# The second layer's gate product made behind the gate, into the head's weighted input

## The chip, the cores and the metric

The program runs on one core of a Trainium2 chip. The metric is the device time of one execution in microseconds (us), the median of several runs. A profile is one further execution, taken by the hardware profiler: its span runs from the first to the last instruction, and its own time includes what lies around the span.

## The reference, cut to what matters

The program is a network of four layers in float32. The change lies in the second, which takes an image of 56 x 56 points (3136 tokens), two images of a batch, 128 channels. The channels are cut into four heads of 32, which are computed one behind another, since each takes the result of the one before as part of its input:

```python
chunks = jnp.split(x, 4, axis=3)
prev = _vss_block(chunks[0], p) + vss_skip * chunks[0]
outs = [prev]
for i in range(1, 4):
    s = prev + chunks[i]
    prev = _vss_block(s, p) + vss_skip * s
    outs.append(prev)
x_res = cvm_skip * x_orig + jnp.concatenate(outs, axis=3)
return _layernorm(x_res, final_ln_w, final_ln_b)

def _vss_block(x, p):
    return x + _ss2d(_layernorm(x, p['ln1_w'], p['ln1_b']), p)

def _ss2d(x, p):
    xx, z = jnp.split(x @ in_proj_w.T, 2, axis=-1)
    xx = silu(depthwise_conv_3x3(xx) + conv_b)
    y = ...                                   # four scans over the image
    y = _layernorm(y, out_norm_w, out_norm_b) * silu(z)
    return y @ out_proj_w.T
```

So a head's result is (1 + vss_skip) * s + ((y - mean) / sd * w + b) * silu(z) @ out_proj. The last term falls into two: one with w that needs y, and one with the norm's bias b, which is (b * silu(z)) @ out_proj and needs only the gate silu(z). This second product is what the change moves. In the data given b is zero and w is one, but the kernel takes both as inputs and computes both products.

## The kernel before, in words

Engines: PE is TensorE, DVE VectorE, ACT ScalarE, POOL GpSimd; SP issues the transfers.

The second layer is the class `Layer1`. A head's scans take both images at once: 2 x 64 inner channels fill 128 partitions, and 3136 tokens lie along the free axis. Between the scans of one head and those of the next lies a stretch of work in chunks of 448 tokens (8 rows of the image, 4 tiles of 112 tokens), seven chunks in all. Only these stretches are touched. There are five: one before the first head's scans, three between heads, and one behind the last head, in which the third layer also begins.

`run` sets the order of emission: for each head it emits the scans, then for c from 0 to 7 first `after(head - 1, c)`, which ends the head before, and then `before(head, c)`, which prepares the next. For head 0, `before` alone is called (through `start`), and behind head 3 `after` with the last normalisation (`last`) and the work that follows. The inside of the scans is an order written out by hand; the stretches between are put into each engine's queue by the compiler's scheduler, whose result differs from the order of emission.

Buffers that matter: `self.prev` holds the head's running input (tokens in the partitions; the profile calls it pair), `self.z` the gate in channel layout (also in a buffer named pair), `self.row` and `self.col` the convolution's results in two orders, `self.y` the scans' sum, `k.X` the layer's input and result (X). `self.R["vss_skip"]` already holds 1 + vss_skip. `self.outs[0]` and `self.outs[1]` are the output matrix multiplied by w and by b (outonw and outonb).

`before(head, c)`, by lines:

- L842: prev += X (the next head's input); L78 to L86: its norm over 32 channels, with DVE, ACT and, at L86, POOL.
- L848, L849: POOL multiplies X by cvm_skip and prev by 1 + vss_skip. `after` later adds the head's product to it.
- L852: four transposes of nrm into a PSUM tile pt; L853: ACT copies it to hT; L855: in-projection of the convolution's half; L856: ACT writes it into the padded image pad.
- `conv_rows` for chunk c - 1 (it needs the row below): on DVE as one L464 and eight L466, or on PE as nine matmuls with diagonal weights (L460; 18 passes in the trace, an f32 matmul being two). Then L467 (silu, ACT) and L468 (POOL, a transposed copy). In heads 1 to 3 the calls c = 2, 4, 5, 6 are DVE's and 1, 3, 7 PE's; in head 0, 2 to 6 are DVE's.
- L867: in-projection of the gate's half; L868: silu into z.
- After c == 2 the first steps of the next scans are begun.

`after(head, c)`: L881 squares y (ACT), L883 multiplies y by the gate (POOL, yc), L888 makes the gate's product with outs[1], L890 the variance, L892 the product of yc with outs[0], L894 and L895 the reciprocal deviation; then on DVE L899 u = p2 + prev, L903 t = p1 * rs, L907 prev = t + u, and on POOL L908 X += prev. In head 3, POOL adds X to u (L901) and L905 writes t + u into X.

PSUM: [...] `pmid1` holds two of each of pt, p and pv (one for head 0, where only pt is used); `pcon1` has two pcv. In SBUF the pool mid1 has two of each of its tiles.

Behind a stretch, the next scans' first broadcast (L364, PE) and product (L417, DVE) start the scan (L358, DVE).

Of the kernel before, what the change touches and what calls it, by code (L numbers as in the profile page):

```python
# [14 lines left out]
F32 = mybir.dt.float32  # L15
BF16 = mybir.dt.bfloat16
AF = mybir.ActivationFunctionType
ALU = mybir.AluOpType
# [3 lines left out]
B = 2  # L22
# [3 lines left out]
TP = 112  # L26
NT = L // TP
CH = 448
# [42 lines left out]
def layernorm_tokens(k, out, x, sq, st, d, by=None, last="POOL"):  # L71

    nc = k.nc
    g = x.shape[1]
    mean, var = st[:, 0, :], st[:, 1, :] if by is None else by
    nc.vector.tensor_reduce(mean, x, AX.X, ALU.add)  # L78
    nc.vector.tensor_scalar_mul(mean, mean, 1.0 / d)
    nc.vector.tensor_tensor(out, x, mean.unsqueeze(2).to_broadcast([TP, g, d]), ALU.subtract)  # L80
    nc.scalar.activation(sq, out, AF.Square)
    nc.vector.tensor_reduce(var, sq, AX.X, ALU.add)
    nc.scalar.activation(var, var, AF.Sqrt, bias=k.eps[:TP], scale=1.0 / d)
    nc.vector.reciprocal(var, var)
    if last == "POOL":
        nc.gpsimd.tensor_tensor(out, out, var.unsqueeze(2).to_broadcast([TP, g, d]), ALU.mult)  # L86
    else:
        for i in range(g):
            nc.scalar.activation(out[:, i], out[:, i], AF.Copy, scale=var[:, i : i + 1])
# [21 lines left out]
class Scans:  # L111
# [290 lines left out]
    def emit(self, s):  # L402
        nc = self.k.nc
        now, one, two, three = (self.at(s + i) for i in range(4))
        before, done = self.at(s - 1), self.at(s - 2)
        if s == len(self.steps) + 2:
            self.take_out(self.steps[-1]["job"])
# [5 lines left out]
        if before:  # L413
            self.keep(before)
# [31 lines left out]
def conv_rows(k, pools, pad, diag, taps, bias, row, col, c, by):  # L446


    nc = k.nc
    sp, pp = pools  # L450
    cs = slice(CH * c, CH * (c + 1))

    def shifted(t):
        dy, dx = divmod(t, 3)
        return pad[:, 8 * c + dy : 8 * c + dy + 8, dx : dx + HW]

    if by == "PE":
        s = pp.tile([128, CH], F32, name="pcv")
        for t in range(9):
            nc.tensor.matmul(s, lhsT=diag[:, t, :], rhs=shifted(t), start=t == 0, stop=t == 8)  # L460
    else:
        s = sp.tile([128, CH], F32, name="cv")
        v = s.rearrange("p (r w) -> p r w", w=HW)
        nc.vector.tensor_scalar(v, shifted(0), taps[:, 0:1], None, ALU.mult)  # L464
        for t in range(1, 9):
            nc.vector.scalar_tensor_tensor(v, shifted(t), taps[:, t : t + 1], v, ALU.mult, ALU.add)  # L466
    nc.scalar.activation(row[:, cs], s, AF.Silu, bias=bias)  # L467
    nc.gpsimd.tensor_copy(  # L468
        col.rearrange("p (w h) -> p w h", h=HW)[:, :, 8 * c : 8 * c + 8],
        row[:, cs].rearrange("p (h w) -> p w h", w=HW),  # L470
    )
# [87 lines left out]
def layer0(k, d, big, follow):  # L559
# [3 lines left out]
    with ExitStack() as ctx:  # L563
# [46 lines left out]
        with ExitStack() as sctx:  # L610
# [87 lines left out]
            for b in range(B):  # L698
                with ExitStack() as bctx:
# [23 lines left out]
                    for c in range(NCH + 1):  # L723
                        if b == 0 and c == 2:
                            norm(1, (ap, tp), groups)
                        if b > 0 and c < NCH:
                            after(b - 1, (sp, pp, ip), c, *outs)
                        before(b, (sp, cp), c, pads, diag)
                        if c == 2:
                            scans.first(cp)  # L730
                scans.run()
        with ExitStack() as bctx:
            sp = bctx.enter_context(k.pool("midl", 2))
            pp = bctx.enter_context(k.pool("pmidl", psum=True))
            ip = bctx.enter_context(k.pool("onel"))
            outs = outputs(ip)
            chunk = follow(bctx)
            for c in range(NCH + 1):
                if c < NCH:
                    after(B - 1, (sp, pp, ip), c, *outs)  # L740
                chunk(c)


class Layer1:
# [4 lines left out]
    D = 32  # L749
# [80 lines left out]
    def before(self, head, pools, c, pad):  # L830


        k, nc, D, W = self.k, self.k.nc, self.D, self.W
        sp, pp, vp = pools
        cs = slice(CH * c, CH * (c + 1))
        if c < NCH:
            sv = self.chunk(self.prev, c)
            xs = self.chunk(self.channels(head), c)
            if head == 0:
                nc.vector.tensor_copy(sv, xs)  # L840
            else:
                nc.vector.tensor_tensor(sv, sv, xs, ALU.add)  # L842
            nrm = sp.tile([TP, 4, B * D], F32, name="nrm")
            nv = nrm.rearrange("p j (b c) -> p (j b) c", c=D)
            sq = sp.tile([TP, 4 * B, D], F32, name="sq")
            st = sp.tile([TP, 2, 4 * B], F32, name="st")
            layernorm_tokens(k, nv, sv, sq, st, D)
            nc.gpsimd.tensor_scalar(xs, xs, self.R["cvm_skip"], None, ALU.mult)  # L848
            nc.gpsimd.tensor_scalar(sv, sv, self.R["vss_skip"], None, ALU.mult)  # L849
            pt = pp.tile([2 * D, CH], F32, name="pt")  # L850
            for i in range(4):
                nc.tensor.transpose(pt[:, TP * i : TP * (i + 1)], nrm[:, i], k.ident[:TP, :TP])  # L852
            nc.scalar.copy(self.hT[:, cs], pt)  # L853
            ps = vp.tile([128, CH], F32, name="pcv")
            nc.tensor.matmul(ps, lhsT=W["in_w"][:, 0, :], rhs=self.hT[:, cs], start=True, stop=True)  # L855
            nc.scalar.activation(  # L856
                pad[:, 1 + 8 * c : 9 + 8 * c, 1 : 1 + HW], ps.rearrange("p (r w) -> p r w", w=HW),
                AF.Identity, bias=self.inb[:, 0:1],
            )
        if c > 0:  # L860
            conv_rows(
                k, (sp, vp), pad, self.diag, W["taps"], W["conv_b"], self.row, self.col, c - 1,
                "DVE" if c in ((2, 3, 4, 5, 6) if head == 0 else (2, 4, 5, 6)) else "PE",
            )
        if c < NCH:
            ps = vp.tile([128, CH], F32, name="pcv")
            nc.tensor.matmul(ps, lhsT=W["in_w"][:, 1, :], rhs=self.hT[:, cs], start=True, stop=True)  # L867
            nc.scalar.activation(self.z[:, cs], ps, AF.Silu, bias=self.inb[:, 1:2])  # L868
        if c == 2:
            self.scans.first(vp)  # L870

    def after(self, head, pools, c):

        k, nc, D = self.k, self.k.nc, self.D
        sp, pp = pools
        cs = slice(CH * c, CH * (c + 1))
        y, gate = self.y[:, cs], self.z[:, cs]
        sq = sp.tile([128, CH], F32, name="sq0")  # L880
        nc.scalar.activation(sq, y, AF.Square)  # L881
        yz = sp.tile([128, CH], F32, name="yc0")
        nc.gpsimd.tensor_tensor(yz, y, gate, ALU.mult)  # L883
        p = pp.tile([TP, 2, 4, B * D], F32, name="p")
        pv = pp.tile([TP, 4 * B], F32, name="pv")
        tiles = [slice(TP * i, TP * (i + 1)) for i in range(4)]
        for i, ts in enumerate(tiles):
            nc.tensor.matmul(p[:, 1, i], lhsT=gate[:, ts], rhs=self.outs[1], start=True, stop=True)  # L888
        for i, ts in enumerate(tiles):
            nc.tensor.matmul(pv[:, B * i : B * (i + 1)], lhsT=sq[:, ts], rhs=self.mean, start=True, stop=True)  # L890
        for i, ts in enumerate(tiles):
            nc.tensor.matmul(p[:, 0, i], lhsT=yz[:, ts], rhs=self.outs[0], start=True, stop=True)  # L892
        rs = sp.tile([TP, 4 * B], F32, name="rs")
        nc.scalar.activation(rs, pv, AF.Sqrt, bias=k.eps[:TP])  # L894
        nc.vector.reciprocal(rs, rs)  # L895
        p1, p2 = (p[:, i].rearrange("p j (b c) -> p (j b) c", c=D) for i in range(2))
        s, x = self.chunk(self.prev, c), self.chunk(self.channels(head), c)
        u = sp.tile([TP, 4 * B, D], F32, name="u")
        nc.vector.tensor_tensor(u, p2, s, ALU.add)  # L899
        if head == 3:  # L900
            nc.gpsimd.tensor_tensor(u, u, x, ALU.add)  # L901
        t = sp.tile([TP, 4 * B, D], F32, name="t")
        nc.vector.tensor_tensor(t, p1, rs.unsqueeze(2).to_broadcast([TP, 4 * B, D]), ALU.mult)  # L903
        if head == 3:
            nc.vector.tensor_tensor(x, t, u, ALU.add)  # L905
        else:
            nc.vector.tensor_tensor(s, t, u, ALU.add)  # L907
            nc.gpsimd.tensor_tensor(x, x, s, ALU.add)  # L908

    def last(self, sp, c):  # L910
# [548 lines left out]
class Mixer:  # L1459
# [104 lines left out]
    def into(self, by, place, onto=None):  # L1564
# [3 lines left out]
        for outs in sorted(by, key=len):  # L1568
            ps = self.product(by[outs])
            for o in outs:  # L1570
# [4 lines left out]
                else:  # L1575
                    nc.vector.tensor_tensor(place(o), onto(o), ps, ALU.add)

    def unit(self, f0, eo, after, later, project):


# [463 lines left out]
```

## Time and profile before

| what | value |
|---|---|
| median of 3 runs (lowest, highest) | 9105.64 us (9102.32, 9109.07) |
| the profiled execution's own time | 9098.37 us |
| its span | 9096.6 us |
| PE busy (share of the span) | 7993.2 us (88%) |
| PE weight loads | 4765.5 us (52%) |
| DVE busy | 7088.0 us (78%) |
| POOL busy | 6350.1 us (70%) |
| ACT busy | 3854.8 us (42%) |
| moved by DMA | 1362.92 MB |
| the stretch before head 0's scans | 2748.7 to 2883.7 us, 135.0 us |
| the stretch head 0 to 1 | 3519.5 to 3615.9 us, 96.4 us |
| the stretch head 1 to 2 | 4248.9 to 4345.6 us, 96.7 us |
| the stretch head 2 to 3 | 4983.4 to 5079.7 us, 96.3 us |
| the end of head 3's last scan | 5719.0 us |

The busy shares are averages over four layers with different limits. The stretches that the change touches are some 6% of the span, so these shares say little on it; the windows cut at the scans do. The ends of a stretch are taken as the end of a head's last scan instruction (L358) and the start of the next head's first.

### The profile page before, as it was taken

The page shows a single profiled execution, that of the slowest core. Times are in us where ns is not written, and L with a number is a line of the kernel's source. Part 1 is how long each engine was busy: PE and PEld are TensorE (multiplying, and loading weights), DVE is VectorE, ACT ScalarE, POOL GpSimd, SP SyncE. Part 2 cuts the span into 40 slices and gives each one's busy share as a digit, 9 for nine tenths or more (in the row PEclk, how much of TensorE's full clock was granted, in tenths as well). Part 3 has the DMA queues.
Part 4 walks back from the last instruction along what each step waited for, and adds up shares of the span by engine and source line. Part 5 has one row for each costly group of instructions (what it writes and reads, how often), then busy time and mean ns, then how long its engine had stood idle before and what let it go on. Part 6 is the DMA issues. An engine that isn't in the chain of part 4 may idle for free. (4 is left out here: it accounts for less than half of the span.)

```text
span 9096.6 us, 93496 instructions
## 1 busy us (share of the span) xinstructions
PE 7993.2 (88%) x28687; PEld 4765.5 (52%) x28687; DVE 7088.0 (78%) x7568; ACT 3854.8 (42%) x6644; POOL 6350.1 (70%) x4066
## 2 busy tenths in 40 slices
PE   8888888888887888888888888699999999999998
PEld 4444445444444444444444444355688888874555
DVE  8999998999997997998999899511467667665442
ACT  4555545555555555554554555433211111114331
POOL 6999996999996997998899799566311111115551
PEclk9999999999999998998999899799999999999999
DMA  5666664666664995996898699100233333320004
GB/s 159 221 221 220 222 212 127 221 221 220 222 220 110 230 226 134 227 228 157 203 227 204 157 227 224 39 3 3 85 96 105 104 94 110 93 63 8 14 1 135
DMA packets 780368, 1362.92 MB, mean 150 GB/s; under 512 B 133101, under 2 KB 405486, under 8 KB 779834
## 3 DMA queue, kind: packets, MB, share of 16 engines
q1 hardware_dynamic: 779866, 1356.95, 53.1%
q8 instruction: 227, 3.72, 0.2%
q14 instruction: 275, 2.25, 0.1%
HBM read 1317.03 MB, written 39.60 MB: 149 GB/s over the span
## 5 line engine op out<-in xcount | busy, mean ns | idle before, releaser
L430 POOL TENSOR_TENSOR p<-h,c 128x784 f32<-128x784 f32 x2048 | 3761.2, 1864 | 115.0 <-DVE h L358 33.1
L358 DVE TENSOR_TENSOR_SCAN h<-a,state,h 128x784 f32<-128x784 f32 x1536 | 2791.8, 1840 | 51.6 <-ACT a L339 28.7
L378 PE MATMUL acc<-p,center 128*128 128x392 f32 x4096 | 1499.0, 499 | 22.7 <-POOL p L430 20.8
L378 PE MATMUL acc<-p,ident 128*128 128x392 f32 x4096 | 1491.9, 498 | 6.7 <-POOL p L430 6.7
L417 DVE TENSOR_TENSOR h<-du,b 128x784 f32<-128x784 f32 x1408 | 1336.7, 949 | 75.6 <-PE b L364 70.4
L339 ACT ACTIVATE a<-delta,L0A 128x784 f32<-128x784 f32 x1024 | 939.3, 918 | 973.4 <-DVE h L358 971.5
L339 ACT ACTIVATE a<-delta,L1A 128x784 f32<-128x784 f32 x1024 | 939.2, 917 | 908.3 <-DVE h L358 905.3
L364 PE MATMUL b<-three,sel 96*128 96x512 bf16 (+1 forms) x2816 | 728.6, 341 | 563.9 <-DVE h L417 460.1
L433 POOL TENSOR_TENSOR h<-du,b 128x784 f32<-128x784 f32 x640 | 1190.3, 1860 | 4.1 <-PE pcv L460 4.1
L378 PEld LDWEIGHTS acc<-p,center 128*128 128x128 f32 x4096 | 740.9, 192 | 536.8 <-POOL p L430 60.2
L378 PEld LDWEIGHTS acc<-p,ident 128*128 128x128 f32 x4096 | 743.9, 192 | 512.8 <-POOL p L430 26.5
L1089 POOL TENSOR_TENSOR total<-total,e 128x448 f32<-128x448 f32 (+1 forms) x644 | 735.6, 1142 | 326.0 <-ACT e L1078 286.0
L358 DVE TENSOR_TENSOR_SCAN h<-a,h 128x784 f32<-128x784 f32 x512 | 901.7, 1780 | 36.7 <-ACT a L339 21.1
L364 PEld LDWEIGHTS <-sel 96*128 96x128 bf16 x2816 | 281.5, 100 | 1230.9 <-issue 1048.6
L1572 DVE TENSOR_TENSOR u<-u,cv 128x512 f32<-128x512 f32 x1024 | 623.7, 681 | 326.6 <-PE cv L1559 325.4
L1603 POOL TENSOR_TENSOR u<-u,S 128x1024 f32<-128x1024 f32 x64 | 150.0, 2365 | 1041.0 <-DVE S L1572 1041.0
L1078 ACT ACTIVATE e<-sc 128x448 f32<-128x448 f32 (+1 forms) x700 | 377.2, 543 | 723.0 <-PE sc L1076 596.3
L1574 ACT COPY u<-cv 128x512 f32<-128x512 f32 x256 | 149.5, 587 | 829.3 <-PE cv L1559 775.7
L1673 PE MATMUL pj<-u,Wm 128*128 128x196 f32 (+8 forms) x1536 | 354.7, 384 | 5.7 <-DVE A L1679 5.7
L1076 PE MATMUL sc<-big 128*128 128x448 f32 (+1 forms) x700 | 323.4, 547 | 15.4 <-ACT e L1078 12.3
L1070 PE MATMUL av<-e,big 128*128 128x448 f32 (+1 forms) x700 | 320.9, 545 | 1.2 <-DVE e L1083 1.0
L1653 POOL TENSOR_TENSOR both<-mpm 128x512 f32<-128x512 f32 x32 | 40.6, 1269 | 392.3 <-DVE Wm L1709 272.8
(452 smaller groups left out, 11251.1 us busy)
## 6 DMA issues: line engine op xcount, KB each, us to landing
c<-rows SPq DMA_DIRECT2D x1024, 392.0 KB, 4.0
c<-rows SPq DMA_DIRECT2D x2048, 196.0 KB, 4.8
b<-rows SPq DMA_DIRECT2D x320, 392.0 KB, 4.5
b<-rows SPq DMA_DIRECT2D x640, 196.0 KB, 4.6
H<-raw SPq DMA_DIRECT2D x32, 1568.0 KB, 7.6
wC<-win SPq DMA_DIRECT2D x64, 576.0 KB, 6.4
w<-in_L_weight_dram SPq DMA_DIRECT2D x52, 512.0 KB, 6.3
wA<-win SPq DMA_DIRECT2D x64, 384.0 KB, 5.6
```

What stands on the lines that cost most here:

```text
L339: self.k.nc.scalar.activation(x["a"], g["delta"][ci], AF.Exp, scale=self.w["A"](g["kd"], ci, x["n"]))
L358: self.k.nc.vector.tensor_tensor_scan(h, a, h, start, ALU.mult, ALU.add)
L364: self.k.nc.tensor.matmul(ps[:, c0:c1], lhsT=self.w["selB"](x["n"]), rhs=x["g"]["three"][:, c0:c1], start=True, stop=True)
L378: nc.tensor.matmul(job["acc"][:, i, 0:392], lhsT=self.w["sum"], rhs=x["p"][:, 392 * i : 392 * (i + 1)], start=False, stop=n == NS - 1,)
L417: nc.vector.tensor_tensor(one["h"], one["g"]["du"][one["ci"]], one["b"], ALU.mult)
L430: nc.gpsimd.tensor_tensor(now["p"], now["h"], now["c"], ALU.mult)
L433: nc.gpsimd.tensor_tensor(three["h"], three["g"]["du"][three["ci"]], three["b"], ALU.mult)
L1076: nc.tensor.matmul(ps[:n], lhsT=keys[b][:, KT * j : KT * j + n], rhs=q, start=True, stop=True)
L1078: nc.scalar.activation(e[:n], ps[:n], AF.Exp, scale=scale)
L1089: nc.gpsimd.tensor_tensor(total[:n], total[:n], e[:n], ALU.add)
L1572: nc.vector.tensor_tensor(place(o), place(o), ps, ALU.add)
L1673: nc.tensor.matmul(ps[:, lo - c0 : hi - c0], lhsT=Ws[f][:, eo, r, :], rhs=u[:, b, f, lo - a0 : hi - a0], start=f == 0, stop=f == 1,)
```

## The change

In `before`, behind the gate's silu of a chunk, four matmuls with outs[1] write the gate's product into a second tile of the buffers pt. One DVE instruction then sets prev to prev * (1 + vss_skip) + product; it takes the place of POOL's multiplication (L849). In head 3 POOL adds X to that at once. In `after`, the four matmuls with outs[1] and the addition u = p2 + prev are gone (in head 3 also POOL's addition): t = p * rs is added to prev directly. p has one product in place of two, still in one bank. The tile pt now has 128 partitions, since it serves both uses.

The diff does one thing more: in heads 1 to 3 the call c = 5 of the convolution (chunk 4 counted from 0) is taken from DVE's list and goes to PE.

```diff
@@ before
             nc.gpsimd.tensor_scalar(xs, xs, self.R["cvm_skip"], None, ALU.mult)
-            nc.gpsimd.tensor_scalar(sv, sv, self.R["vss_skip"], None, ALU.mult)
-            pt = pp.tile([2 * D, CH], F32, name="pt")
+            pt = pp.tile([128, CH], F32, name="pt")[: 2 * D]
             for i in range(4):
                 nc.tensor.transpose(pt[:, TP * i : TP * (i + 1)], nrm[:, i], k.ident[:TP, :TP])
             nc.scalar.copy(self.hT[:, cs], pt)
...
-                "DVE" if c in ((2, 3, 4, 5, 6) if head == 0 else (2, 4, 5, 6)) else "PE",
+                "DVE" if c in ((2, 3, 4, 5, 6) if head == 0 else (2, 4, 6)) else "PE",
             )
         if c < NCH:
             ps = vp.tile([128, CH], F32, name="pcv")
             nc.tensor.matmul(ps, lhsT=W["in_w"][:, 1, :], rhs=self.hT[:, cs], start=True, stop=True)
             nc.scalar.activation(self.z[:, cs], ps, AF.Silu, bias=self.inb[:, 1:2])
+
+            p = pp.tile([128, CH], F32, name="pt")[:TP, 0 : 4 * B * D]
+            for i in range(4):
+                ts = slice(CH * c + TP * i, CH * c + TP * (i + 1))
+                nc.tensor.matmul(
+                    p[:, B * D * i : B * D * (i + 1)], lhsT=self.z[:, ts], rhs=self.outs[1], start=True, stop=True
+                )
+            nc.vector.scalar_tensor_tensor(
+                sv, sv, self.R["vss_skip"], p.rearrange("p (j c) -> p j c", c=D), ALU.mult, ALU.add
+            )
+            if head == 3:
+                nc.gpsimd.tensor_tensor(sv, sv, xs, ALU.add)
@@ after
-        p = pp.tile([TP, 2, 4, B * D], F32, name="p")
+        p = pp.tile([TP, 512], F32, name="p")[:, 0 : 4 * B * D]
         pv = pp.tile([TP, 4 * B], F32, name="pv")
         tiles = [slice(TP * i, TP * (i + 1)) for i in range(4)]
         for i, ts in enumerate(tiles):
-            nc.tensor.matmul(p[:, 1, i], lhsT=gate[:, ts], rhs=self.outs[1], start=True, stop=True)
-        for i, ts in enumerate(tiles):
             nc.tensor.matmul(pv[:, B * i : B * (i + 1)], lhsT=sq[:, ts], rhs=self.mean, start=True, stop=True)
         for i, ts in enumerate(tiles):
-            nc.tensor.matmul(p[:, 0, i], lhsT=yz[:, ts], rhs=self.outs[0], start=True, stop=True)
+            nc.tensor.matmul(
+                p[:, B * D * i : B * D * (i + 1)], lhsT=yz[:, ts], rhs=self.outs[0], start=True, stop=True
+            )
         rs = sp.tile([TP, 4 * B], F32, name="rs")
         nc.scalar.activation(rs, pv, AF.Sqrt, bias=k.eps[:TP])
         nc.vector.reciprocal(rs, rs)
-        p1, p2 = (p[:, i].rearrange("p j (b c) -> p (j b) c", c=D) for i in range(2))
         s, x = self.chunk(self.prev, c), self.chunk(self.channels(head), c)
-        u = sp.tile([TP, 4 * B, D], F32, name="u")
-        nc.vector.tensor_tensor(u, p2, s, ALU.add)
+        t = sp.tile([TP, 4 * B, D], F32, name="t")
+        nc.vector.tensor_tensor(
+            t, p.rearrange("p (j c) -> p j c", c=D), rs.unsqueeze(2).to_broadcast([TP, 4 * B, D]), ALU.mult
+        )
         if head == 3:
-            nc.gpsimd.tensor_tensor(u, u, x, ALU.add)
-        t = sp.tile([TP, 4 * B, D], F32, name="t")
-        nc.vector.tensor_tensor(t, p1, rs.unsqueeze(2).to_broadcast([TP, 4 * B, D]), ALU.mult)
-        if head == 3:
-            nc.vector.tensor_tensor(x, t, u, ALU.add)
+            nc.vector.tensor_tensor(x, t, s, ALU.add)
         else:
-            nc.vector.tensor_tensor(s, t, u, ALU.add)
+            nc.vector.tensor_tensor(s, s, t, ALU.add)
             nc.gpsimd.tensor_tensor(x, x, s, ALU.add)
```

In instructions of the program: DVE has 28 L899 less and 28 of the new multiply-and-add more, three L464 and 24 L466 less; PE has 27 more matmuls at L460 and 112 gate matmuls in another place; POOL has 28 L849 less.

## The prediction

> **What bounds the kernel now.** I read the windows of the trace first, cut where one scan ends and the next begins, because the change touches only the stretches between scans. Four stretches lie behind a head's scans, one before the first head's; inside the scans no instruction moves.
>
> ```profile
> 2748.70:2883.70 135.00, 106.23 (x512) 67.77 (x512) 85.17 (x159) 82.74 (x119) 62.50 (x66) 0.90 0.14 34
> 3519.50:3615.90 96.40, 84.40 (x302) 53.76 (x302) 49.94 (x111) 49.34 (x81) 45.00 (x50) 0.73 0.14 32
> 4248.90:4345.60 96.70, 84.81 (x302) 53.77 (x302) 49.84 (x110) 49.22 (x81) 45.15 (x50) 0.74 0.13 32
> 4983.40:5079.70 96.30, 84.28 (x302) 53.65 (x302) 49.95 (x111) 49.22 (x81) 45.39 (x50) 0.73 0.13 32
> 5719.00:5830.00 111.00, 59.65 (x264) 46.64 (x264) 79.42 (x130) 62.74 (x162) 48.27 (x33) 0.58 0.03 7
> ```
>
> The columns are length, then busy time of PE, PEld, DVE, ACT, POOL, then PE's granted clock. In the three middle stretches PE is busy 84 of 96 us and DVE 50: PE is the engine with least to spare. The clock says why so few matmuls take so long: it is 0.5 in the small products and full in the convolutions.
>
> ```profile
> 4266.00:4272.00 6.00, 6.00 (x34) 6.00 (x34) 4.13 (x10) 0.73 (x2) 3.92 (x5) 0.50 0.01 3
> 4296.00:4302.00 6.00, 6.00 (x18) 2.64 (x17) 2.06 (x7) 0.75 (x3) 1.39 (x2) 1.00 0.00 0
> 4332.00:4338.00 6.00, 4.88 (x6) 2.01 (x7) 5.96 (x9) 5.94 (x8) 1.01 (x1) 0.57 0.09 20
> ```
>
> Next the groups of the middle stretch (4248.9 to 4345.6, my model for all three), by shape; the trace counts two passes for an f32 matmul:
>
> ```profile
> L460 PE MATMUL pcv<-pad,diag 128*128 128x448 f32 x54 | 24.8, 620 | 0.0
> L466 DVE SCALAR_TENSOR_TENSOR cv<-pad,L1taps,cv 128x448 f32<-128x448 f32 x32 | 22.3, 718 | 3.7 <-ACT pad L856 3.1
> L888 PE MATMUL p<-outonb,pair 128*112 128x64 f32 x56 | 10.7, 358 | 0.0
> L868 ACT ACT_TABLE_LOAD x3 | 3.8, 1283 | 0.9 <-PE pcv L867 0.9
> L899 DVE TENSOR_TENSOR u<-p,pair 112x256 f32<-112x256 f32 x7 | 2.9, 413 | 18.8 <-PE p L892 18.8
> ```
>
> Last the timeline at the end of that stretch, PE and then DVE (start, duration):
>
> ```profile
> 4323.51 1.02 PE L867 MATMUL pcv<-big,L1in_w 64*128 64x448 f32 x2
> 4324.45 0.96 PE L852 MATMUL pt<-ident,nrm 112*64 112x112 f32 x8
> ...
> 4334.90 9.40 PE L460 MATMUL pcv<-pad,diag 128*128 128x448 f32 x18
> 4344.15 0.50 PE L364 MATMUL b<-three,sel 96*128 96x512 bf16 x2
> ```
> ```profile
> 4318.50 0.98 DVE L223 TENSOR_TENSOR du<-delta,big 128x784 f32<-128x784 f32 x1 [1.97 <-ACT delta L214]
> ...
> 4341.58 0.96 DVE L417 TENSOR_TENSOR h<-du,b 128x784 f32<-128x784 f32 x1
> 4344.75 0.97 DVE L417 TENSOR_TENSOR h<-du,b 128x784 f32<-128x784 f32 x1 [2.20 <-PE b L364]
> 4345.64 3.46 DVE L358 TENSOR_TENSOR_SCAN h<-a,h 128x784 f32<-128x784 f32 x2
> ```
>
> The reader is to see a near tie. DVE convolves until 4341.6; PE's last convolution (18 passes, 9.4 us at a cold clock) ends at 4344.3 and the next broadcast (L364) ends the wait of the second L417, then the scan starts. PE sets the end by 2.2 us. PE is also far ahead with transposes: chunks 6 and 7 are transposed together at 4324.5, while chunk 5's convolution is DVE's.
>
> [...] the trace has 1283, and the next activation starts 0.01 us behind it, so I use 1.28. [...] 112x256 adds take no longer with an operand in PSUM (L899, 0.41 us) than from SBUF alone (L907, 0.49).
>
> **The change part by part**, in the middle stretch unless said. Chunks are 1 to 7; "gate product" is the 4 matmuls by outs[1]. The built order of the changed kernel's instructions was read on each engine.
>
> Removed behind the scans: 28 gate products, 56 passes. 16 passes of them were free already: they ran at 4250.2 to 4253.2, under the scan's last sums. 24 stood among the 15 groups of 8 passes between 4257.5 and 4279.8 (22.3/15 = 1.49 us a group), 16 beside the first in-projections. Now 13 groups stand ahead of the first transpose: 4257.5 + 13 x 1.49 = 4276.9. POOL ends later: its 7th yc follows product 5 (4273.9), then come two L848 and one L908 of 0.92 and 0.72, then L86: 4278.3, against 4280.3 before. Gain 2.0. L899 (7 x 0.41) goes from DVE, which idles 47 us here: nothing, except in the last stretch.
>
> POOL's L849 (7 x about 1.0) goes: POOL is idle half of the stretch, nothing. Its multiplication moves into the new DVE instruction, 7 of 112x256 from PSUM. No row shows this form: between the 0.41 of L899, an add of that size from PSUM, and the 0.72 of the larger L466, which is the same operation; I take 0.45, 3.2 us in all, beside PE. Behind it on DVE's queue stand L80 of the chunk after next and convolution taps. Head 3's POOL addition (7 x 0.72) is hidden in the same idle time.
>
> Moved, though the few words don't tell it: chunk 5's convolution goes from DVE (9 x 0.72 = 6.5 us off) to PE (18 passes: 7.0 us at full clock as at 4316.5, 8.4 at 4292.5, 9.4 at 4334.9; I take 8.4). PE has 12 us idle in the stretch.
>
> Added in front: per chunk in-projection, silu, gate product (8 passes: 0.9 us at full clock, as L892 at 4302.6; 1.5 at half). In the built order the gate product of chunk k precedes the transpose of chunk k+1, and the two share the two pt banks. Walk: first convolution starts at 4289.7 (before 4292.5), since of the removed groups 4.5 us stood here and one gate product (1.5) and its silu came; the third (chunk 3's) ends at 4319.4 (before 4323.6), because the 4.17 us wait on chunk 5's transpose is gone: it now stands behind this convolution. Gain so far 4.2. From there nothing overlaps:
> - in-projection 1.0, silu 0.7, gate product 1.0, transpose 0.5: chunk 5 is transposed at 4322.6 (before at 4311);
> - copy to SBUF 0.6, L855 and L867 2.0; the silu of chunk 5 stands on ACT behind a table load, a square root, the pad and another load and ends at 4327.8; product, 4328.7; chunk 6's transpose, 4329.2;
> - copy 0.65, L855 1.0, convolution 5 8.4, L867 1.0, silu 0.7, product 1.0, transpose 7 0.5: 4342.5;
> - copy 0.65, L855 and L867 2.0, convolution 7 with the last product inside it 8.0: 4353.1;
> - L364 stands behind it: L364 0.6, L417 1.05, L364 0.65, L417 1.0: the scan starts at 4356.4, against 4345.6.
>
> That is +10.8 a stretch. Bounds: PE's instructions alone, without one wait from 4319.4, are 26.6, plus 3.3 to the scan: 4349.3, +3.7; at half clock throughout, +15. Three stretches: 3 x 10.8 = +32.4 (11 to 45).
>
> First stretch (head 0): 7 additions of 0.45 on DVE, five of them where it is busy: 2.2; in the tail the last gate product stands inside the last convolution at half clock, 8 x 0.2 = 1.6; the single pt bank makes transpose k+1 wait for addition k, which the 13 us between chunks hide; one wait of DVE for a silu, 1.2. Sum +5 (-2 to +14).
>
> Last stretch (after head 3): PE loses 56 passes and nothing is added; DVE, busiest here with 79 of 111, loses 2.9; its 3.2 us wait for POOL's L901 goes, and about 1 us of order. -7 (-15 to 0).
>
> Sum: +5 + 32.4 - 7 = +30. The profiled execution spans 9096.6 us and took 9098.4 as a whole; it would take 9128. It lies 7 below the median 9105.6 of the runs, so the forecast is 9105.6 + 30 = 9136.
>
> **Rivals.** Serial PE tail as walked: 9136.
>
> DVE was the tail: then 6.5 us less convolution less some 1.5 of additions brings the scan forward 5 us in three stretches, -15, and with -7 behind head 3: 9084, faster. For it: DVE convolves without a pause from 4327 to 4341.6. Against: L364 of PE ends the wait. It decides if PE is through its last convolution before 4344.3, which needs 12 us less than my walk.
>
> PE's waits fill up: chunks overlap, +3.7 x 3, the first +2, the last -9: +4, 9110, no change that counts. For it: PE has 12 us of idle time; against: all of it is waits that the new order multiplies.
>
> Cold chain: [...] +15 x 3, first stretch +14: with -4 it is +55, 9161.
>
> **Numbers.** Serial tail 0.55, cold chain 0.18, waits filled 0.20, DVE tail 0.07. About 0.2% (18 us) is what the measurement of this kernel tells from no change: slower 0.73, same 0.20, faster 0.07. The range 9104 to 9164 takes in the cold chain and the filled waits.
>
> **What would show it.** Gaps between scans of about 107 us in place of 96 three times, about 140 for 135, some 113 for the last 120; in the tail PE idle behind "ACT pair" at the gate products, chunk 6's transpose some 5 us later than 4324, and L364 right behind a convolution. DVE idle before its first L417 by over 5 us. I am wrong if the three gaps are shorter than 96, or if the scans themselves change length.

## The result and the profile after

The changed kernel takes 9147.17 us (median of 5, 9140.96 to 9159.44) against 9102.32 us before (5 runs): the ratio is 1.0055, interval 1.0044 to 1.0066, so 40 to 60 us more. A second set of runs gave 1.0054 (1.0042 to 1.0067). Slower was forecast, by 30 us; the forecast of 9136 is 11 us under the median, within its range.

The windows of the changed kernel's trace, cut as before where scans end and begin. The columns are again length, then busy time of PE, PEld, DVE, ACT and POOL, then PE's granted clock and what the DMA moved:

```profile
2745.20:2894.90 149.70, 125.88 (x568) 83.81 (x568) 90.80 (x166) 78.72 (x116) 52.66 (x59) 0.83 0.13 32
3532.10:3644.90 112.80, 94.50 (x320) 56.95 (x320) 45.52 (x102) 50.15 (x81) 38.43 (x44) 0.74 0.11 27
4280.00:4389.00 109.00, 92.00 (x320) 55.17 (x320) 45.43 (x102) 50.15 (x81) 38.50 (x44) 0.77 0.12 28
5029.70:5139.60 109.90, 92.83 (x320) 55.26 (x319) 46.09 (x100) 50.13 (x81) 43.64 (x51) 0.75 0.12 28
5778.30:5889.30 111.00, 50.11 (x208) 37.42 (x208) 74.73 (x125) 63.01 (x162) 47.74 (x26) 0.57 0.02 7
```

The three middle stretches went from 96.3, 96.7 and 96.2 us to 112.7, 108.9 and 109.9. The first went from 135.0 to 149.7. PE's busy time in a middle stretch rose by 7 to 10 us; in the second of them 6.7 of 7.2 us is chunk 5's convolution (L460, 31.5 us for 24.8, 18 more passes). The rest of the stretch, in which PE waits, rose from 12 to 17 or 18 us. The groups of the stretch from 4280.0 to 4389.0 show both, and the new operations' prices:

```profile
L460 PE MATMUL pcv<-pad,diag 128*128 128x448 f32 x72 | 31.5, 592 | 0.0
L466 DVE SCALAR_TENSOR_TENSOR cv<-pad,L1taps,cv 128x448 f32<-128x448 f32 x24 | 17.1, 712 | 3.4 <-ACT pad L855 2.9
L872 PE MATMUL pt<-outonb,pair 128*112 128x64 f32 x56 | 8.5, 306 | 5.1 <-ACT pair L867 5.1
L875 DVE SCALAR_TENSOR_TENSOR pair<-pair,L1vss_skip,pt 112x256 f32<-112x256 f32 x7 | 3.3, 478 | 16.6 <-PE pt L872 16.6
```

L872 is the gate product in its new place (L888 before) and L875 the new DVE instruction, 0.478 us each. PE waits 5.1 us in this stretch for the gate ("ACT pair L867"). The timeline of PE at the end of the stretch (start, duration, engine, line; in brackets the idle time before, and what ended it):

```profile
4351.81 1.02 PE L866 MATMUL pcv<-big,L1in_w 64*128 64x448 f32 x2
4353.55 1.00 PE L872 MATMUL pt<-outonb,pair 128*112 128x64 f32 x8 [0.72 <-ACT pair L867]
4354.38 0.55 PE L851 MATMUL pt<-ident,nrm 112*64 112x112 f32 x4
4355.55 1.02 PE L854 MATMUL pcv<-big,L1in_w 64*128 64x448 f32 x2 [0.61 <-ACT big L852]
4356.40 0.91 PE L866 MATMUL pcv<-big,L1in_w 64*128 64x448 f32 x2
4359.99 1.09 PE L872 MATMUL pt<-outonb,pair 128*112 128x64 f32 x8 [2.67 <-ACT pair L867]
4360.88 0.95 PE L851 MATMUL pt<-ident,nrm 112*64 112x112 f32 x4
4362.44 1.86 PE L854 MATMUL pcv<-big,L1in_w 64*128 64x448 f32 x2 [0.61 <-ACT big L852]
4364.23 8.68 PE L460 MATMUL pcv<-pad,diag 128*128 128x448 f32 x18
...
4379.92 6.23 PE L460 MATMUL pcv<-pad,diag 128*128 128x448 f32 x16
4385.99 0.50 PE L364 MATMUL b<-three,sel 96*128 96x512 bf16 x2
```

The same order repeats for each chunk: in-projection of the gate (L866), gate product (L872) once the silu is there, and only then the next chunk's transposes (L851), a wait for their copy, the next in-projection. No chunk's transposes run ahead of the product of the chunk before. PE waits for the silu in five of the seven chunks, from 0.27 to 2.67 us. On DVE, at the end of this stretch:

```profile
4386.53 0.97 DVE L417 TENSOR_TENSOR h<-du,b 128x784 f32<-128x784 f32 x1 [5.71 <-PE b L364]
4388.08 0.97 DVE L417 TENSOR_TENSOR h<-du,b 128x784 f32<-128x784 f32 x1 [0.58 <-PE b L364]
4388.97 3.46 DVE L358 TENSOR_TENSOR_SCAN h<-a,h 128x784 f32<-128x784 f32 x2
```

DVE now has nothing to do for 5.71 us before the first product of the scan; before, it convolved until 4341.6 and the near tie with PE was 2.2 us. PE alone sets the end.

### The profile page after: what moved, and what is told of

Same layout as the page of the kernel before. It is cut to its first block, busy times and chain, and to the rows that moved or that the text cites. A ratio compares the mean times of both kernels' runs of the same rounds, so it can differ in the third digit from the quotient of the medians.

```text
span 9157.7 us, 93579 instructions
## 1 busy us (share of the span) xinstructions
PE 8049.7 (88%) x28741; PEld 4792.7 (52%) x28741; DVE 7072.5 (77%) x7541; ACT 3852.2 (42%) x6641; POOL 6318.5 (69%) x4038
## 5 line engine op out<-in xcount | busy, mean ns | idle before, releaser
L417 DVE TENSOR_TENSOR h<-du,b 128x784 f32<-128x784 f32 x1408 | 1337.6, 950 | 96.5 <-PE b L364 91.7
```

The lines of the kernel that those rows point to most:

```text
L417: nc.vector.tensor_tensor(one["h"], one["g"]["du"][one["ci"]], one["b"], ALU.mult)
```

## The experiments

Each table entry is a stretch between scans in us, from that kernel's trace; the means are over the three middle stretches. The scans themselves took 633 to 641 us each; the four of a kernel add up to 2546 and 2547 us in the two profiles of before, to 2552 and 2555 in those of the changed kernel, and to 2544 to 2554 in the others.

| kernel | first | 0 to 1 | 1 to 2 | 2 to 3 | middle, mean |
|---|---|---|---|---|---|
| before | 135.0 | 96.3 | 96.7 | 96.2 | 96.4 |
| before_again | 142.7 | 95.2 | 94.8 | 94.7 | 94.9 |
| changed | 149.7 | 112.7 | 108.9 | 109.9 | 110.5 |
| after_again | 149.2 | 112.3 | 111.3 | 112.8 | 112.1 |
| conv_on_pe | 134.9 | 96.5 | 99.8 | 99.9 | 98.7 |
| gate_only | 149.8 | 106.6 | 106.1 | 106.0 | 106.2 |
| own_bank | 149.7 | 99.0 | 99.9 | 99.0 | 99.3 |
| late_gate_dve | 159.4 | 101.6 | 98.9 | 97.4 | 99.3 |
| head0_only | 149.5 | 90.9 | 95.9 | 96.3 | |
| own123_dve | 149.1 | 107.0 | 98.6 | 96.8 | |
| in_scan | 149.0 | 92.9 | 91.2 | 92.6 | 92.2 |

Below, "before" for a middle stretch is 95.65, the mean of the two profiles (96.4 and 94.9), and the changed kernel is 111.3 (110.5 and 112.1): +15.7 a stretch, 47 us in all.

### The two halves of the change apart

conv_on_pe is the kernel before with one edit:

```diff
-                "DVE" if c in ((2, 3, 4, 5, 6) if head == 0 else (2, 4, 5, 6)) else "PE",
+                "DVE" if c in ((2, 3, 4, 5, 6) if head == 0 else (2, 4, 6)) else "PE",
```

> The kernel before, with only chunk 5's convolution of heads 1 to 3 on PE (calls c = 2, 4, 6 on DVE); the gate product stays behind the scans. Serial-tail theory: the transposes still run ahead, so the 18 passes (8.4 us) are added to PE less the 2.8 us of waits that they fill: the three middle stretches take about 102 us each in place of 96.4, the first and last stretch as before, the total is 15 to 18 us above before. Rival (the whole loss of the changed kernel is this convolution): stretches of 109 to 112 as in the changed kernel, total +42. Second rival (DVE was the tail): stretches of 91 to 94, faster by some 10 us.

Measured: 9119.36 us against 9111.68, ratio 1.0011 (1.0003 to 1.0020). The middle stretches are 98.7, +3.1: less than the 102 expected, and far from the 109 to 112 of the first rival. The total is 8 us above before where 15 to 18 was expected. The second rival (DVE was the tail) falls: in stretch 1 to 2 DVE is busy 5.9 us less (43.95 for 49.84) and the stretch is no shorter. Two lines of PE near the end of that stretch before, and then the same place in conv_on_pe, show why 18 passes more cost so little:

```profile
4330.62 1.02 PE L855 MATMUL pcv<-big,L1in_w 64*128 64x448 f32 x2 [1.33 <-ACT pad L856]
4333.12 1.85 PE L867 MATMUL pcv<-big,L1in_w 64*128 64x448 f32 x2 [1.49 <-ACT pair L868]
```
```profile
4318.99 8.21 PE L460 MATMUL pcv<-pad,diag 128*128 128x448 f32 x18
...
4331.65 7.06 PE L460 MATMUL pcv<-pad,diag 128*128 128x448 f32 x18
4338.65 1.02 PE L867 MATMUL pcv<-big,L1in_w 64*128 64x448 f32 x2
4339.59 0.51 PE L364 MATMUL b<-three,sel 96*128 96x512 bf16 x2
4340.37 1.02 PE L855 MATMUL pcv<-big,L1in_w 64*128 64x448 f32 x2 [0.27 <-ACT big L467]
4341.23 0.91 PE L867 MATMUL pcv<-big,L1in_w 64*128 64x448 f32 x2
4342.11 7.03 PE L460 MATMUL pcv<-pad,diag 128*128 128x448 f32 x18
```

The added convolution (4331.65) takes 7.06 us where PE had waited 1.33 and 1.49 us and now waits 0.27, and PE's clock stays full behind it (1.00 from 4321.66 to 4343.66, where before it is 0.50 from 4333 to 4339): the last convolution takes 7.03 us instead of 9.40, the in-projection ahead of it 0.91 instead of 1.85. So 7.06 - 2.6 (waits) - 2.4 - 0.9 = 1.2 of the 3.1 that this stretch took more than before's 96.7. The other 1.9 lie ahead of the added convolution and go with the clock, which is 0.50 up to 4320.66 here and 1.00 from 4316 before: chunk 3's convolution (4318.99) took 8.21 us instead of 7.03, the in-projection ahead of it 1.86 instead of 1.20.

gate_only is the changed kernel with that edit taken back:

```diff
-                "DVE" if c in ((2, 3, 4, 5, 6) if head == 0 else (2, 4, 6)) else "PE",
+                "DVE" if c in ((2, 3, 4, 5, 6) if head == 0 else (2, 4, 5, 6)) else "PE",
```

> The changed kernel with chunk 5's convolution back on DVE (calls 2, 4, 5, 6), so the gate's move alone. Serial-tail theory: each gate product still stands ahead of the next transpose, but the 8.7 us convolution between transposes 6 and 7 goes: middle stretches of about 102 us, total some 12 to 17 us above before, with a first stretch of 140 to 145 and about 4 us gained behind head 3. Rival (the loss is the convolution): stretches of 96 or less, total equal to before or below.

Measured: 9141.15 us against 9111.68, ratio 1.0032 (1.0021 to 1.0044). The middle stretches:

```profile
3525.40:3632.00 106.60, 87.13 (x302) 53.91 (x302) 51.06 (x111) 52.63 (x83) 38.77 (x43) 0.73 0.12 29
4270.20:4376.30 106.10, 89.09 (x302) 54.67 (x302) 51.18 (x110) 52.72 (x83) 38.40 (x43) 0.71 0.13 29
5014.50:5120.60 106.10, 89.15 (x302) 54.81 (x302) 53.81 (x111) 52.64 (x83) 45.92 (x50) 0.71 0.13 29
```

They are 106.2, +10.6, with the same 302 passes as before: the same work in another order. PE is busy 3 to 5 us longer on these passes than before and waits 17 to 19.5 us where it waited 12. 102 was expected, with a total 12 to 17 us above before; it is 29 above. The convolution alone is worth less and the order more than either theory had. The two halves, 3.1 and 10.6, make 13.7 of the 15.7.

### What in the move costs: the shared banks

own_bank gives the gate product of heads 1 to 3 a PSUM tile of its own and, to make room, puts pv into p's bank (so it does two things at once):

```diff
-            p = pp.tile([128, CH], F32, name="pt")[:TP, 0 : 4 * B * D]
+            p = pp.tile([128, CH], F32, name="p2" if head else "pt")[:TP, 0 : 4 * B * D]
...
-        p = pp.tile([TP, 512], F32, name="p")[:, 0 : 4 * B * D]
-        pv = pp.tile([TP, 4 * B], F32, name="pv")
+        both = pp.tile([TP, 512], F32, name="p")
+        p, pv = both[:, 0 : 4 * B * D], both[:, 4 * B * D : 4 * B * D + 4 * B]
```

> The changed kernel with PSUM banks of its own for the gate product in heads 1 to 3 (the variance pv moves into the bank of p to make room); the convolution stays on PE. In the built order two or more chunks' transposes stand ahead of a gate product again. Serial-tail theory with the shared pt banks as the cause: middle stretches of 100 to 104 us, total some 25 us under the changed kernel. Rival (the amount of PE work, not the chain, sets the stretch): 108 to 111 us, total as the changed kernel.

Measured: 9122.29 us against 9111.68, ratio 1.0012 (1.0006 to 1.0019). Windows of the middle stretches, and PE at the end of the second of them:

```profile
3529.80:3628.80 99.00, 86.42 (x320) 53.35 (x319) 43.15 (x100) 47.94 (x79) 38.65 (x44) 0.79 0.14 31
4264.70:4364.60 99.90, 87.34 (x320) 54.32 (x320) 43.10 (x101) 47.81 (x79) 39.09 (x44) 0.78 0.13 31
5000.90:5100.00 99.10, 86.47 (x320) 53.42 (x320) 44.68 (x102) 47.94 (x79) 45.01 (x51) 0.79 0.13 31
```
```profile
4338.47 0.57 PE L851 MATMUL pt<-ident,nrm 112*64 112x112 f32 x4
4338.97 1.02 PE L854 MATMUL pcv<-big,L1in_w 64*128 64x448 f32 x2
4339.92 1.00 PE L872 MATMUL p<-outonb,pair 128*112 128x64 f32 x8
4340.84 1.02 PE L866 MATMUL pcv<-big,L1in_w 64*128 64x448 f32 x2
4341.70 0.91 PE L854 MATMUL pcv<-big,L1in_w 64*128 64x448 f32 x2
4342.59 1.00 PE L872 MATMUL p<-outonb,pair 128*112 128x64 f32 x8
4343.42 6.99 PE L460 MATMUL pcv<-pad,diag 128*128 128x448 f32 x18
```

The stretches are 99.3, 12.0 less than with the shared banks and as much work; the total is 25 us under the changed kernel's, as expected, and the stretches a little below the expected 100 to 104. The last transposes (4338.5) now stand ahead of four gate products (two of them shown), PE has no wait from chunk 3's convolution (4330.56) until the scan's first broadcast, and chunk 5's convolution takes 6.99 us at full clock (1.00 from 4330.71 to 4357.71; 8.68 above, with 0.50 up to 4367). Set against the first profile of the changed kernel (110.5), PE waits 12.6 us a stretch in place of 17.5 and is busy 86.7 us in place of 93.1 with the same 320 passes: 4.9 us of the gain is waiting, and 6.4 is that more passes met the full clock (the clock column has 0.79 for 0.75). Against conv_on_pe, which has the same convolutions on PE, the moved product costs 0.6 us a stretch. So it was not the product that cost, but its place in PE's queue ahead of the next transposes, which came with the tile name that it shares with them. The rival (the amount of PE work) falls. How the scheduler gets from the shared name to that order was not looked into.

late_gate_dve keeps the shared banks, but emits the product of chunk c - 1 at the end of `before` of chunk c, as a function `gate` with the body of the diff; the convolution is DVE's as before:

```diff
+        if c > 0:
+            self.gate(head, pp, c - 1)
         if c == 2:
             self.scans.first(vp)
```

> The changed kernel with the gate product of a chunk emitted one chunk later, behind the next chunk's transposes and in-projections, and with chunk 5's convolution on DVE as before. Serial-tail theory: the products then fill PE's waits and nothing waits for a gate; the middle stretches take 94 to 98 us, the total is 0 to 8 us under before (4 us from behind head 3, less what the first stretch loses). Rival (28 gate products ahead of a scan cost their PE time wherever they stand): stretches of 101 to 104, total some 15 us above before.

Measured: 9134.30 us against 9111.68, ratio 1.0026 (1.0018 to 1.0035). The middle stretches are 99.3 (101.6, 98.9, 97.4), +3.6: in the middle between what I expected and the rival. With the same two banks and the same convolutions as gate_only, another order is worth 6.9 us a stretch, which speaks for the order as the cause. The first stretch takes 159.4, 9.6 more than gate_only's: head 0 has one pt bank for both uses, so that a late product holds up the transposes behind it (argued from the code, not tried apart). The total is a miss: 23 us above before where 0 to 8 under was expected.

own123_dve leaves head 0 as before, gives the product of heads 1 to 3 one bank and lets the seven pv of a stretch share one:

```diff
+                self.pv = ctx.enter_context(k.pool("pv1", psum=True)).tile([TP, NCH, 4 * B], F32, name="pv")
+                if head < 4:
+                    self.gp = ctx.enter_context(k.pool("pg1", psum=True))
...
-        pv = pp.tile([TP, 4 * B], F32, name="pv")
+        pv = self.pv[:, c]
```

> Heads 1 to 3 only make their gate product in front, in a PSUM bank of its own (the seven pv of a stretch share one bank to make room), the convolution of chunk 5 on DVE, head 0 as before. Serial-tail theory with the shared bank as cause: first stretch 135 us, middle stretches 94 to 98, the stretch behind head 3 some 4 us shorter, total 2 to 8 us under before. Rival (products in front cost their PE time even with room): middle stretches of 99 to 101 us, total 4 to 9 us above before.

Measured: 9128.50 us against 9109.61, ratio 1.0020 (1.0012 to 1.0029). The stretches 1 to 2 and 2 to 3 are 98.6 and 96.8, on average 2.0 above before, between what was expected and the rival: with its own bank and the old convolution the moved product neither gains nor loses much. They are 8.4 shorter than the same two of gate_only, which has the same convolutions; here pv has a bank of its own, so this second way of making room bears own_bank out. Stretch 0 to 1 has head 0's products still behind the scan and head 1's already in front, 358 passes for 302, and takes 107.0, 11.2 more. The total is a miss: 19 us above before where 2 to 8 under was expected; those 11 us are part of it, the rest is not accounted for.

### What removing the products is worth, and the first stretch

head0_only makes only head 0's products in front:

```diff
+            if head in (0,):
+                self.gate(head, pp, c)
```

> The gate product made in front of the scans for head 0 alone (into the pt bank, as in the changed kernel); heads 1 to 3 as before, with the convolution on DVE. It tells whether the first stretch's loss belongs to head 0's products. Theory A: the first stretch is about 150 us again, with PE at half clock from 11 to 25 us behind the scan's end, the other stretches 94 to 97, total 11 to 16 us above before. Theory B (the half clock in four profiles of four was chance): about 143 us, total 5 to 9 us above before.

Measured: 9109.10 us against 9109.61, ratio 1.0002 (0.9994 to 1.0011). One line of the windows, stretch 0 to 1:

```profile
3533.20:3624.00 90.80, 75.76 (x246) 43.93 (x246) 48.28 (x102) 49.43 (x81) 45.17 (x50) 0.76 0.13 34
```

Without the 56 passes this stretch takes 90.9, 4.8 less than before: more than the 2.0 that the prediction gave it. The first stretch is 149.5, as theory A had it, but the total fits neither theory: no more than before, where A expected 11 to 16 us and B 5 to 9. Whether the 149.5 is head 0's product could not be told from one profile, because of what before_again showed:

> The kernel before again: first stretch 135 us and middle stretches 96 to 97, total within 5 us of before. If the clock of the first stretch is chance, it may stand at half here, with a stretch of 141.

It is the kernel before once more, 9112.33 us against 9109.61 (ratio 1.0000, 0.9992 to 1.0008). Its windows:

```profile
2746.40:2889.10 142.70, 114.19 (x512) 74.51 (x512) 84.27 (x160) 83.16 (x119) 63.05 (x67) 0.84 0.14 34
3528.70:3623.90 95.20, 83.22 (x302) 52.27 (x302) 49.90 (x111) 49.22 (x81) 45.34 (x50) 0.75 0.13 32
4259.50:4354.40 94.90, 82.98 (x302) 52.05 (x302) 49.94 (x111) 49.21 (x81) 45.14 (x50) 0.75 0.15 32
4990.20:5084.90 94.70, 82.81 (x302) 52.17 (x302) 49.85 (x110) 49.22 (x81) 45.11 (x50) 0.75 0.14 32
```

The first stretch takes 142.7 us where the first profile had 135.0, with the same instructions in the same order on every engine, and the clock column says 0.84 where it said 0.90. Two lines of PE's timeline, some 12 us behind the scan's end, first of before_again, then of before:

```profile
2758.66 0.75 PE L509 MATMUL p<-out_w,z 128*112 128x128 f32 x2
2759.20 1.70 PE L491 MATMUL pm<-pair,avg 128*128 128x448 f32 x2
```
```profile
2760.74 0.45 PE L509 MATMUL p<-out_w,z 128*112 128x128 f32 x2
2761.03 0.92 PE L491 MATMUL pm<-pair,avg 128*128 128x448 f32 x2
```

PE's granted clock is 0.51 from 2757.4 to 2770.4 in before_again, and 1.00 from 2759.7 to 2772.7 in before.

So I summed, for every kernel, the time at half clock in the first stretch, from windows of 1 us:

| first stretch | kernels | length, us | at half clock, us |
|---|---|---|---|
| code as before | before, conv_on_pe | 135.0, 134.9 | 27.3, 27.3 |
| code as before | before_again | 142.7 | 44.4 |
| code as before | own123_dve, in_scan | 149.1, 149.0 | 61.4, 61.5 |
| product in front | changed, after_again, head0_only, gate_only, own_bank | 149.2 to 149.8 | 51.2 each |
| product one chunk later | late_gate_dve | 159.4 | 64.9 |

In all five profiles of code as before the order on every engine is the same. The length follows the half-clock time at (149.1 - 135.0) / (61.4 - 27.3) = 0.41 us per us. At 51.2 us that gives 144.9, and the kernels with the product in front take 149.6: by this estimate the product itself costs 4.7 us there. In head0_only this is what the next stretch gains, and the total is even. That the five kernels with the product in front all met the same 51.2 us while the unchanged code met three values, I can't explain; so it is open whether the half-clock time itself belongs to the change.

> The changed kernel again, beside the others on the same chip: how far stretches and scans repeat. Expected: first stretch 143 to 150 us, middle stretches 109 to 113, scans within 3 us of the first profile, total 40 to 50 us above before. If the half clock at the first stretch's start is bound to this program it is there again; if it is chance it may be gone.

after_again: 9160.25 us against 9109.61, ratio 1.0054 (1.0042 to 1.0067); the stretches are in the table, and the scans are within 4.2 us of the first profile's, where 3 was expected.

### A place where the products are hidden

in_scan is the kernel before with the products inside the scans: at step 44 + 32 c of a head's 256 the four matmuls of chunk c go into the broadcasts' PSUM tile, and ACT copies them to SBUF, where L899 finds them.

```diff
+        for j, f in enumerate(getattr(self, "extra", ())):
+            self.pieces.setdefault((44 + 32 * j, 0), []).append((0, 0, f, ()))
...
+        for i in range(4):
+            o, t = B * self.D * i, CH * c + TP * i
+            self.k.nc.tensor.matmul(
+                ps[:TP, 0, o : o + B * self.D], lhsT=self.z[:, t : t + TP], rhs=self.outs[1], start=True, stop=True
+            )
+        self.k.nc.scalar.copy(self.p2[c], ps[:TP, 0, 0 : 4 * B * self.D])
...
-            nc.tensor.matmul(p[:, 1, i], lhsT=gate[:, ts], rhs=self.outs[1], start=True, stop=True)
```

> The kernel before, with the gate products neither behind nor in front of the scans but inside them: one chunk's four matmuls at every 32nd step of a head's 256, into the bank of the broadcasts, copied to SBUF by ACT; behind the scans DVE adds the copy in place of p2. The convolution stays on DVE. If removing the 56 passes behind the scans is worth what head 0's variant showed (a stretch of 90.9 us where 94.7 to 96.7 is usual) and the scans hide the products: middle stretches of 90 to 92 us, the stretch behind head 3 some 4 us shorter, first stretch as before (135 to 149 by its clock), scans within 2 us of before, total 10 to 20 us under before. Rival (each product holds back a broadcast, which holds the scan): scans 7 x 1.5 = 10 us longer each, total 20 to 30 us above before.

Measured: 9100.47 us against 9111.04, ratio 0.9988 (0.9981 to 0.9995): the one version under before.

```profile
3528.90:3621.80 92.90, 77.56 (x246) 46.38 (x246) 54.27 (x110) 49.54 (x81) 45.30 (x50) 0.72 0.13 33
4257.80:4349.00 91.20, 75.81 (x246) 45.19 (x246) 54.54 (x111) 49.54 (x81) 45.56 (x50) 0.74 0.15 34
4983.40:5076.00 92.60, 77.24 (x246) 46.34 (x246) 54.35 (x111) 49.53 (x81) 45.39 (x50) 0.72 0.14 33
```

The middle stretches are 92.2, 3.5 less each, and the four scans 636.1, 636.0, 634.4 and 637.4 us, in sum 2544 where the two profiles of before have 2546 and 2547: seven products with a copy each are hidden there. The rival (each holds back a broadcast) falls. Three stretches by 3.5 are about the 10.6 us between the medians. The gain expected behind head 3 is not in its profile, where the next layer's attention starts 144.9 us behind the last scan (140.7 before) and the rest of the program takes some 7 us longer; why, stays open, and so the agreement of the 10 us with the medians may be chance.

## Why the prediction was right, and by how much it missed

The walk. The serial chain of the middle stretch held step by step. That no matmul passes a product that waits for its gate was my assumption; in the trace each of PE's five waits for the silu (0.27 to 2.67 us) ends with the product, and the next chunk's transposes stand behind it. A table load on ACT, taken at 1.28 us, is 1.283 in both traces. In us from the end of the scan, predicted and in the trace: first convolution starts at 40.8, 40.2; chunk 3's ends at 70.5, 71.8; chunk 5 is transposed at 73.7, 74.9; chunk 6 at 80.3, 81.8; chunk 7 at 93.6, 95.9; the last convolution ends at 104.2, 106.1; the scan starts at 107.5, 108.9. The trace is 1.3 us late when chunk 3's convolution ends: from the start of the first convolution this took 31.7 us, 29.7 in the walk, with waits and matmuls at half clock (chunk 3's gate product took 1.76 us at a clock of 0.50, chunk 2's 1.00 us at 1.00) that were not told apart. Another 1.1 comes between the transposes of chunks 6 and 7, from matmuls at half clock (0.50 from 4361 to 4367) that I had faster: L854 behind chunk 6's copy took 1.86 (1.0 assumed), the convolution 8.68 (8.4). The end was then faster than walked. In the same stretch the walk gave +10.8 and the first two profiles +12.2.

The size. Three stretches were to cost 32.4 and cost 47 (15.7 each over two profiles a side). Of the 4.9 us a stretch, 1.0 is that the profile I walked was a long one (96.7 against a mean of 95.65), 1.4 the walk's own miss, and 2.4 that the other five stretches are longer than the one compared above: 109.9 to 112.8 us, at half clock for 54.6 to 58.0 us where that one has 51.2. This is the rival of the cold chain, in part: more of these stretches ran at half clock, and the same passes took longer. It was a share of the loss, not another outcome.

One reading ahead of the walk was too simple. The prediction put the clock at 0.5 in the small products and full in the convolutions. In the same trace the clock stands at 0.50 in every window of 6 us from 4260 to 4290, four of these five with PE busy throughout; the first and the last of them are

```profile
4260.00:4266.00 6.00, 6.00 (x34) 6.00 (x33) 2.53 (x9) 2.87 (x7) 2.97 (x3) 0.50 0.00 0
4284.00:4290.00 6.00, 6.00 (x16) 2.92 (x15) 3.03 (x9) 4.07 (x5) 3.57 (x4) 0.50 0.00 1
```

In windows of 1 us the clock is at 1.00 up to 4257, at 0.50 from 4258 to 4295 and at 1.00 again from 4296: the first convolution (4292.5) met 0.50 for its first 3 us, the last one (4334.9, 9.40 us) for nearly 5, and eight passes of L892 at 4302.6, small products, took 0.91 us at 1.00. The sums do not rest on that reading, since they took the times of single matmuls from the trace. It bears on the cold chain, which was my estimate for half clock throughout (+15 a stretch): here half clock stood for 38 us with PE idle for 1.0 of them (0.51 and 0.53 ahead of the first two transposes), so that waits in it do not explain its length.

The parts of the walk were not right in proportion. I priced the convolution's move at 8.4 us of PE, which alone costs 3.1 (conv_on_pe); the move of the product alone costs 10.6 (gate_only), where 102 us, some 6 more than before, was expected when it ran. The first was 3 us less than expected and the second 4.6 more, so the walk was a good account of the whole and a poor one of its halves; that these two errors offset each other is luck.

The bound without waits, +3.7 a stretch, is about what own_bank shows: +3.6 with no wait on PE from chunk 3's convolution on. So the rival "PE's waits fill up" is what the same edit does with a bank of its own (+11 us in the medians; 9110 was named for it, +4, with a last stretch that gains more). It was given 0.20 for waits that the order multiplies; that argument was right for the order as built, and the shared pt banks, which the prediction named in passing, are what made that order.

First stretch. Predicted +5, from -2 to +14; in the profile +14.7. At equal half-clock time it is 4.7 by the estimate above; the three terms of the +5 were not taken apart, so their agreement with it is not shown one by one. The other 10 us go with PE's clock (51.2 us at half clock in place of 27.3). The unchanged code varies as much (134.9 to 149.1), but as all five kernels with the product in front met one value, these 10 us can't be put down to chance for certain.

Last stretch. Predicted -7, from -15 to 0. The start of the attention's first product with its values moved from 140.7 and 140.4 us behind the last scan to 136.4 and 136.9: -3.9. With the same code for this stretch gate_only has 134.9 and own_bank, which differs in pv's bank alone, 139.9. DVE's wait of 3.2 us for POOL is gone, as forecast, and so are the 2.8 us of L899; but DVE's wait for the squares ahead of L82 grew from 0.8 to 6.2 us. Which of the forecast's terms came up short is not shown beyond that.

Removed products. The walk had them save 2.0 us ahead of the first transpose, and 4.2 by the third convolution. With nothing put in front, head0_only's next stretch shows 4.8 and in_scan 3.5 at the end. The gain was real, and was spent behind it.

New DVE instruction. Taken at 0.45, it takes 0.478; it is hidden in the middle as said (DVE idle 16.6 us before it, waiting for PE).

DVE as the tail, 9084: refuted by conv_on_pe, and by the 5.71 us of DVE's wait.

The sum: 47 + 4.7 - 3.9 = 48, against 40 to 60 measured. That it fits is not proof that nothing else changed. The two profiled executions of the changed kernel took 12 and 4 us more than the medians of their sets (9159.44 and 9164.64 us), those of before 7 and 9 less, and on average their spans differ by 62.8 us: 47.0 in the middle stretches, 10.6 in the first, 6.9 in the four scans, -3.9 behind head 3, 5.7 in all that follows, and -3.4 ahead of the first stretch. So the prediction's +32.4 for the middle was mis-sized, and in the profiles the scans and the last layers, which it put at nothing, add to it, whether through this change or not. In a stretch of 75 us of the last layer the changed kernel is at half clock for 30 to 31 us where before, gate_only and own_bank have 18 to 21. It is 33 to 34 us in in_scan and own123_dve too; what it goes with stays open.

## What to carry to other kernels

Before a step is moved ahead, look at which buffers it will take turns with: a step that shares a tile name with the start of the next chunk can end up ahead of that start in the engine's queue, and the pipeline turns into a chain (12.0 us a stretch here, gone with a bank of its own). Read the order of the queue, not only the amount of work. Moving work from behind a bottleneck to in front of it doesn't remove it from the engine that bounds both; here it paid only where that engine had room, inside the scans (-3.5 us a stretch), in which PE is busy 523 to 528 of 633 to 639 us and DVE 613 to 614 (before's windows of the four scans). Try the parts of a change separately: the convolution's move looked like the dear part and was the cheap one.

## What the runs showed of the hardware

A stretch of unchanged code, with the same order on every engine, took from 134.9 to 149.1 us, and its length went with PE's time at half clock (27.3 us in the shortest, 61.4 in the longest). The same instructions met different clocks in two profiles of one kernel: 0.51 over 13 us near the start of that stretch in before_again, 1.00 in before. What sets the clock, and when it changes, was not shown. It follows for reading: two profiles of a stretch with short products are compared with their half-clock times beside them; without that, a difference of up to 14 us in the first stretch, or of 1.5 in a middle one (96.4 and 94.9 for the same kernel), says nothing about a change. In conv_on_pe the convolution moved to PE paid for part of itself, since the one behind it ran at full clock (7.03 us in place of 9.40).
